# The low parts of a split float32 product stored as float16, with bfloat16 views of the weights

## The chip, the cores and the metric

The kernel runs on one core of one Trainium2 chip. The time is the device time of one execution in microseconds. The kernel before was run three times: 698.88 us in the median, 698.78 us the fastest and 699.11 us the slowest.

## The reference, cut to what matters

The input `x` has 2 x 1024 rows of 2048 numbers. Two residual steps follow each other, each a layer norm, a product with a 2048 x 2048 matrix and a gated add:

```python
x = x + tanh(g_xattn[0]) * matmul(fake_quant(layernorm(x)), fake_quant(ctx_4096))
y = layernorm(x)
y = concatenate([y[..., :1638], -4.0 * y[..., 1638:]], axis=-1)
x = x + tanh(g_ffn[0]) * scale * (y @ mask)        # mask: 2048 x 2048 of zeros and ones
```

The first product has operands of 8 bits (`fake_quant` rounds to 0..255). In the second product the left operand is float32 and has to keep more digits than one pass of TensorE gives; the right operand holds small whole numbers.

## The kernel before

Rows are taken in 16 tiles of 128 (`T`), 8 of each batch. Everything that is a matmul contracts 128 rows at a time and makes 128 x 512 numbers in PSUM.

**First product.** Both operands are float16 (lines 544 and 646 of the profile, `acc<-q,q1T`, `acc_M<-q,q1S` and the like). For batch 1 a part of it uses seven half-size products in place of eight.

**Second product.** Two row tiles t and u form a pair p, and there are eight pairs. A pair's normed rows are scaled (`scale2`, line 685), transposed on TensorE in float32 (`turn2`, line 692, four 128 x 128 transposes at a time) and taken out of PSUM as `A` (`take2`). The two tiles by the two halves of the contraction make a 2 x 2 block matrix, the mask likewise, and Winograd's form of Strassen's scheme replaces eight block products by seven, M1 to M7. The left sums are made in place (`combine`, lines 722 to 728), the right sums T1 to T4 are made once from the mask's bytes (`combine_w`, line 767) and kept in DRAM.

Each left operand is split in two: `part_hi` (line 738, ScalarE) rounds `A` to fp32r, the type that TensorE takes in one pass; `part_lo` (line 742, VectorE or GpSimd) stores `A - hi`, also as fp32r. `load_w` fetches a right block as bytes; `widen` (line 782, ScalarE) makes of each 128 x 1024 slice k an fp32r tile `wf`. Its values are whole numbers of at most a few bits.

`mm2` (line 809) does one slice k of one product for one pair. It issues four matmuls: hi with the left 512 columns of `wf`, hi with the right ones, lo with the left, lo with the right. All four add up in PSUM. So the second product is 7 products x 8 pairs x 8 slices x 4 = 1792 matmuls, 896 of them with hi and 896 with lo, in the order hi, hi, lo, lo. Only at the very end (the last four slices of the last pair, `tail`) the order is hi, lo, hi, lo. An fp32r matmul is one instruction that loads its own stationary operand; the profile still shows the load as a LDWEIGHTS row. A float16 matmul is two instructions, a Ldweights and a Matmult. `add2` (line 825) adds the result, times the factor `f2`, to the rows kept in DRAM, and `store2` writes them out.

**What sets the order.** The class `Plan` holds a list of all steps with estimated costs and due times; it simulates the engines and writes down an order for each. The steps are then issued in this order to TensorE, VectorE, ScalarE, GpSimd and the DMA queue of SyncE. The costs are constants in the code (4.2 for one `mm2`), and the change does not touch them. Pairs are taken two at a time (`ops_product2`), the second pair four slices behind the first, so that each `wf` serves two `mm2`, eight matmuls; the parts hi and lo of a product are made while the product before it runs.

**The factors.** `factor` (line 453) makes the layer norm's factor r = 1/sqrt(var + eps) of each row tile; the tiles of the second norm have v equal to "b". `f2` (line 381) is tanh(g_ffn) x scale.

Of the kernel before, what the change touches and what calls it, by code (L numbers as in the profile page):

```python
# [12 lines left out]
F32R = mybir.dt.float32r  # L13
F16 = mybir.dt.float16
BF = mybir.dt.bfloat16
# [3 lines left out]
ALU = mybir.AluOpType  # L19

P = 128
NB = 512
HB = 1024
EPS = 1e-5
UNIT = 2.0**-24
CENTER = 128.0
PAGES = 44

# [251 lines left out]
def gated_xattn_ffn_kernel(  # L280
# [29 lines left out]
    nc = tc.nc  # L310
# [9 lines left out]
    KH = KT // 2  # L320
# [19 lines left out]
    def page(shape, dtype, name: str):  # L340
        return pages.tile([P] + shape, dtype, tag="page", name=name)
# [8 lines left out]
    sc = const.tile([P, 7], F32, name="sc")  # L350
    nc.sync.dma_start(sc, scalars.partition_broadcast(P))
    gate = const.tile([P, 2], F32, name="gate")
# [8 lines left out]
    c1 = const.tile([P, 1], F32, name="c1")  # L361
    nc.vector.tensor_scalar(c1, z1, -1.0, CENTER, ALU.mult, ALU.add)
    c2 = const.tile([P, 1], F32, name="c2")
# [3 lines left out]
    f1u = const.tile([P, 1], F32, name="f1u")  # L367
    nc.vector.tensor_scalar(f1u, f1, 1.0 / UNIT, None, ALU.mult)
    f1c1u = const.tile([P, 1], F32, name="f1c1u")
# [7 lines left out]
    nc.vector.tensor_scalar(kc12d, f1c1, c2, float(K), ALU.mult, ALU.mult)  # L377
    nc.vector.tensor_scalar(kc12, c1, -CENTER, None, ALU.add)
    nc.vector.tensor_scalar(kc12, kc12, f1c2, float(K), ALU.mult, ALU.mult)
    f2 = const.tile([P, 1], F32, name="f2")  # L380
    nc.vector.tensor_scalar(f2, gate[:, 1:2], sc[:, 6:7], None, ALU.mult)

    ident = const.tile([P, P], F32, name="ident")
    make_identity(nc, ident)
# [56 lines left out]
    def factor(v, t: int):  # L441


        va, sd = root.pop((v, t))
        mean = mv[v, t][:, 0:1]
        r0 = small.tile([P, 1], F32, tag="r0", name=f"r0_{v}{t}")
        nc.vector.reciprocal(r0, sd)

        e = small.tile([P, 1], F32, tag="e", name=f"e_{v}{t}")
        nc.vector.tensor_scalar(e, r0, r0, va, ALU.mult, ALU.mult)  # L450
        nc.vector.tensor_scalar(e, e, -0.5, 1.5, ALU.mult, ALU.add)
        r = small.tile([P, 1], F32, tag="r", name=f"r_{v}{t}", bufs=T)
        nc.vector.tensor_scalar(r, r0, e, None, ALU.mult)
        fac[v, t] = (r, mean)
        if v == "a":
            w = small.tile([P, 1], F32, tag="w", name=f"w_{v}{t}")
            nc.vector.tensor_scalar(w, va, r, zs1, ALU.mult, ALU.mult)
            nc.vector.tensor_scalar(w, w, mean, None, ALU.subtract)
            nc.vector.tensor_scalar(r, r, rs1, None, ALU.mult)
            wr = small.tile([P, 1], F32, tag="wr", name=f"wr_{v}{t}")  # L460
            nc.vector.tensor_scalar(wr, w, r, None, ALU.mult)
            fac[v, t] = (r, w, wr)
# [42 lines left out]
    def take1(t: int, h: int, engine=None):  # L505
# [5 lines left out]
        if engine == "ACT":  # L511
            nc.scalar.activation(dst, v, AF.Copy, bias=-CENTER)  # L512
        else:
            nc.vector.tensor_scalar(dst, v, -CENTER, None, ALU.add)  # L514

# [159 lines left out]
    A, hi, lo, wt, wb, wr, wf, back, acc2 = ({} for _ in range(9))  # L675
# [54 lines left out]
    def left(m: str, p: int):  # L730

        t, u = 2 * p, 2 * p + 1
        return {"M1": (t, 0), "M2": (t, 1), "M3": (t, 1), "M4": (u, 1), "M5": (u, 0),
                "M6": (t, 0), "M7": (p, "S3")}[m]
# [3 lines left out]
        nc.scalar.copy(hi[m, p], A[left(m, p)])  # L738

    def part_lo(m: str, p: int, engine=None):  # L740
        lo[m, p] = page([KH, P], F32R, f"lo_{m}_{p}")
        engines[engine].tensor_sub(lo[m, p], A[left(m, p)], hi[m, p].bitcast(F32))  # L742


# [51 lines left out]
    def apart(p: int, m: str):  # L796

        return p == T // 2 - 1 and SUM[m] == "Y"

    def mm2(q: int, m: str, p: int, k: int, js=(0, 1)):  # L800
        if m in OPENS and k == 0 and apart(p, m):
            acc2[SUM[m], p] = [ps_tr.tile([P, NB], F32, tag="tr", name=f"acc2_{m}_{p}_{j}") for j in range(2)]
        elif m in OPENS and k == 0:
            acc = ps_acc.tile([P, 2, NB], F32, tag="acc", name=f"acc2_{m}_{p}")
            acc2[SUM[m], p] = [acc[:, j, :] for j in range(2)]
            acc2[SUM[m], p, 0] = flat(acc)
        for part in (hi, lo):
            for j in js:
                nc.tensor.matmul(  # L809
                    acc2[SUM[m], p][j],  # L810
                    part[m, p][:, k, :],
                    wf[q, m, k][:, ts(j, NB)],
                    start=(m in OPENS and k == 0 and part is hi),
                    stop=(k == KH - 1 and part is lo),
                    skip_group_check=True,
                )

    def load_back(p: int, i: int, h: int):
        back[p, i, h] = page([HB], F32, f"back_{p}_{i}_{h}")
        nc.sync.dma_start(back[p, i, h], kept[2 * p + i, h])  # L820
# [13 lines left out]
    def ops_norm(v: str, t: int, **when):  # L834
        name = lambda kind: ((kind + v, t), 0)
        op({"DVE": 2.0}, variance, v, t, writes=[name("v")], **when,
           reads=[(("bn" + v, t), c) for c in range(NC)])
        op({"ACT": 1.0}, square_root, v, t, reads=[name("v")], writes=[name("sd")], **when)
        op({"DVE": 8.0 if v == "a" else 4.0}, factor, v, t, reads=[name("sd")], writes=[name("r")], **when)
# [187 lines left out]
    def ops_parts(m: str, p: int):  # L1027
        a = ("A",) + left(m, p)
        op({"ACT": ACT(HB)}, part_hi, m, p, reads=both(a), writes=[(("hi", m, p), 0)],
           opens=[("page", ("hi", m, p))], lead=60)  # L1030
        op({"DVE": DV2(HB), "POOL": GPS(HB)}, part_lo, m, p, reads=[*both(a), (("hi", m, p), 0)],
           writes=[(("lo", m, p), 0)], opens=[("page", ("lo", m, p))], lead=60, port=True)
# [20 lines left out]
    def ops_product2(q: int, between):  # L1053
        pairs = (2 * q, 2 * q + 1)
        for n, m in enumerate(ORDER):
# [27 lines left out]
            for i, k, *js in steps:  # L1083
                p = pairs[i]
                js = js[0] if js else (0, 1)
                acc = ("acc2", SUM[m], p)
                two = apart(p, m)
                keys = [(acc + (j,), 0) if two else (acc, j) for j in js]
                opens = [("tr", acc + (j,)) for j in js] if two else [("acc", acc)]
                op({"PE": 2.1 * len(js)}, mm2, q, m, p, k, js, main=True, writes=keys,  # L1090
                   reads=[(("hi", m, p), 0), (("lo", m, p), 0), (("wf", q, m, k), 0)],
                   opens=opens if m in OPENS and k == 0 else [])
                if k == KH - 1:
                    for js2 in [(j,) for j in js] if two else [js]:
                        v = ("back", p) + TAKES[m]
                        keys = [(acc + (j,), 0) if two else (acc, j) for j in js2]
                        op({"DVE": DV2(len(js2) * NB)}, add2, m, p, js2, reads=keys, writes=[(v, j) for j in js2],
                           due=plan.place)
                        if m in LAST:
                            op({"SP": DMA}, store2, p, *TAKES[m], js2, reads=[(v, j) for j in js2], due=plan.place + 60)  # L1100
# [67 lines left out]
    for t in range(TPB, T):  # L1168
        v = ("x", t, 1)
# [60 lines left out]
```

## Time and profile before

| what | value |
|---|---|
| median of three runs | 698.88 us |
| span of the profiled execution, first to last instruction | 697.0 us |
| TensorE (PE) busy with matmuls | 674.0 us, 97% |
| VectorE, ScalarE, GpSimd busy | 490.2, 455.4, 316.8 us |
| granted TensorE clock | 1.000 over the whole span |
| second product's matmul rows | 1792 (896 hi, 896 lo) |
| first product's matmul rows (lines 544, 556, 574, 646) | 1036 |
| hi parts made (line 738) | 56, all on ScalarE |
| lo parts made (line 742) | 56: 30 on VectorE, 26 on GpSimd |

The page gives only the span of the profiled execution, not its time by the clock that the three runs use; the median stands 1.9 us above the span. A group row of the profile reads: line, engine, operation, output<-inputs, shape, count | busy microseconds, mean nanoseconds of one | idle time before them and who ended it. Matmuls are pipelined: a row's duration (389 ns for 512 columns) covers filling and draining, and the next one starts well before its end. What a matmul costs is therefore the distance from its start to the next start.

### The profile page before, as it was taken

The numbers are of one execution on the slowest core, as the hardware profiler recorded it, in microseconds if no ns is written. First come the engines' busy times: TensorE is split into PE (matmuls) and PEld (weight loads), VectorE is DVE, ScalarE is ACT, GpSimd is POOL, SyncE is SP. The second block draws the span as 40 slices with busy tenths as digits, with TensorE's granted clock in tenths as the row PEclk, the third lists the DMA queues.
The fourth block names the chain that finished last, engine by engine and source line by source line (L and its number), as shares of the span: only waits on it lengthen the run. The fifth ranks groups of instructions, "written<-read, shape, count | busy, mean of one in ns | idle before, by whom it ended". The sixth has DMA issues, their size and how long they took to land.

```text
span 697.0 us, 8833 instructions
## 1 busy us (share of the span) xinstructions
PE 674.0 (97%) x3180; PEld 471.7 (68%) x3180; DVE 490.2 (70%) x717; ACT 455.4 (65%) x536; POOL 316.8 (45%) x210
## 2 busy tenths in 40 slices
PE   1999999989999999999999999999999999999997
PEld 0444444468788888878885444447888888888885
DVE  6899958899998886497878888468572425583331
ACT  4599444286888566699926768229699347689540
POOL 8166789863625221855717887975120101040000
PEclk9999999999999999999999999999999999999999
DMA  8999406777995799477379677327074379155032
GB/s 302 393 393 380 162 13 231 259 261 251 361 400 225 233 324 339 140 247 278 120 263 330 222 268 245 121 92 275 27 260 162 105 231 324 67 170 222 22 131 90
DMA packets 63580, 155.78 MB, mean 223 GB/s; under 512 B 4912, under 2 KB 21296, under 8 KB 63536
## 3 DMA queue, kind: packets, MB, share of 16 engines
q1 hardware_dynamic: 63536, 155.21, 62.9%
q8 instruction: 25, 0.41, 0.2%
q14 instruction: 19, 0.16, 0.1%
HBM read 117.44 MB, written 37.75 MB: 223 GB/s over the span
## 4 chain that ended last, share of the span: by engine, by line
PE 87%; DMA 4%; DVE 4%; POOL 2%; ACT 2%; issue 1%; SPq 0%; ACTq 0%; DVEq 0%
PE acc_M L809 57%; PE acc L544 19%; PE acc_M L646 7%; PE tr L692 4%; DMA kv<-in_kv_dram 3%; DMA x<-in_x_dram 1%; POOL x L596 1%; DVE wB L767 1%; ACT wf_M L782 1%; POOL x L592 1%; PE tr L503 1%; DVE qn L472 0%; PE cs L574 0%; DVE x L685 0%; DVE bn_b L426 0%
## 5 line engine op out<-in xcount | busy, mean ns | idle before, releaser
L809 PE MATMUL acc_M<-wf_M,hi_M 128*128 128x512 f32 x896 | 282.0, 395 | 1.6 <-ACT wf_M L782 1.5
L809 PE MATMUL acc_M<-wf_M,lo_M 128*128 128x512 f32 x896 | 277.6, 390 | 0.6 <-POOL lo_M L742 0.6
L782 ACT ACTIVATE wf_M<-wr_M 128x1024 fp32r<-128x1024 uint8 x224 | 221.6, 1050 | 26.8 <-DMA wr_M<-in_wmask_dram 24.2
L809 PEld LDWEIGHTS acc_M<-wf_M,lo_M 128*128 128x128 f32 x896 | 168.0, 188 | 36.8 <-POOL lo_M L742 1.3
L809 PEld LDWEIGHTS acc_M<-wf_M,hi_M 128*128 128x128 f32 x896 | 164.1, 188 | 34.4 <-ACT wf_M L782 3.2
L544 PE MATMUL acc<-q,q1T 128*128 128x512 f16 x768 | 171.6, 381 | 1.2 <-DVE q1T L514 0.8
L825 DVE SCALAR_TENSOR_TENSOR back<-acc_M,f,back 128x1024 f32<-128x1024 f32 (+1 forms) x58 | 72.1, 1245 | 124.7 <-PE acc_M L809 117.1
L742 POOL TENSOR_TENSOR lo_M<-A,hi_M 128x1024 fp32r<-128x1024 f32 x24 | 62.1, 2586 | 179.5 <-ACT hi_M L738 160.1
L544 PEld LDWEIGHTS <-q1T 128*128 128x128 f16 x768 | 75.2, 98 | 90.2 <-issue 1.9
L592 POOL TENSOR_TENSOR x<-x,row 128x512 f32<-128x512 f32 x64 | 88.6, 1408 | 43.8 <-ACT sd_a L438 15.5
L596 POOL TENSOR_TENSOR x<-x,e 128x512 f32<-128x512 f32 x64 | 92.0, 1458 | 30.6 <-ACT e L586 16.1
L738 ACT CAST hi_M<-A 128x1024 fp32r<-128x1024 f32 x48 | 50.1, 1044 | 13.1 <-POOL A L726 4.7
L530 ACT ACTIVATE q<-kv,sc,rs 128x1024 uint8<-128x1024 f32 x45 | 53.5, 1236 | 7.8 <-DMA kv<-in_kv_dram 5.1
L586 ACT ACTIVATE e<-acc,tokb,f1u 128x512 f32<-128x512 f32 x34 | 25.1, 774 | 49.6 <-PE acc L544 47.8
L426 DVE BATCH_NORM_STATS2 bn_b<-x 128x6 f32<-128x512 f32 x64 | 43.1, 684 | 15.9 <-POOL x L596 15.6
L495 ACT COPY A<-tr 128x512 f32<-128x512 f32 x35 | 20.3, 584 | 46.5 <-PE tr L692 45.8
L742 DVE TENSOR_TENSOR lo_M<-A,hi_M 128x1024 fp32r<-128x1024 f32 x24 | 33.7, 1421 | 7.2 <-ACT hi_M L738 7.2
L568 DVE TENSOR_TENSOR pair<-pair,q 128x1024 f16<-128x1024 f16 x36 | 36.6, 1022 | 2.5 <-ACT q L530 0.8
L728 POOL TENSOR_TENSOR A<-A,A 128x1024 f32<-128x1024 f32 x8 | 21.1, 2648 | 23.7 <-DVE A L726 16.4
L522 POOL MEMSET q<- 128x1024 f32 x32 | 29.2, 952 | 5.1 <-DVE q L532 2.2
L512 ACT ACTIVATE q1T<-tr 128x1024 f16<-128x1024 uint8 x22 | 21.3, 1019 | 7.5 <-PE tr L503 6.8
L767 DVE SCALAR_TENSOR_TENSOR wB<-wB,wB 128x2048 uint16<-128x2048 uint16 x8 | 24.2, 3031 | 0.0
(103 smaller groups left out, 594.1 us busy)
## 6 DMA issues: line engine op xcount, KB each, us to landing
kv<-in_kv_dram SPq DMA_DIRECT2D x64, 512.0 KB, 9.2
x<-in_x_dram SPq DMA_DIRECT2D x32, 512.0 KB, 7.7
x<-x SPq DMA_DIRECT2D x32, 512.0 KB, 3.0
back<-x SPq DMA_DIRECT2D x32, 512.0 KB, 6.1
wr_M<-wt_T SPq DMA_DIRECT2D x32, 512.0 KB, 5.6
out_dram<-back SPq DMA_DIRECT2D x30, 512.0 KB, 3.6
wr_M<-in_wmask_dram SPq DMA_DIRECT2D x24, 512.0 KB, 5.4
n<-in_x_dram SPq DMA_DIRECT2D x16, 512.0 KB, 7.2
```

Of the source, the lines that this page charges most:

```text
L426: nc.vector.bn_stats(bn[v, t][:, c, :], xt[src[v, t, c // 2]][:, ts(c % 2, NB)])
L530: nc.scalar.activation(low, v, AF.Identity, bias=z2, scale=rs2)
L544: nc.tensor.matmul(acc1[b, c, tiles[0]][:, i, :], q1T[tiles[i]][:, k, :], rhs1(b, c, k), start=(k == 0), stop=(k == KT - 1),)
L568: nc.vector.tensor_add(colsum[b, c], colsum[b, c], v[:, i : i + 2, :])
L592: nc.gpsimd.tensor_add(xc, xc, colrow[b, c])
L596: nc.gpsimd.tensor_add(xc, xc, ev.pop((t, c)))
L646: nc.tensor.matmul(acc1[key][:, i, :], left_half(p, LEFT1[m])[:, 4 * s + k, :], right1(m, h, s)[:, k, :], start=(m in OPENS and s == 0 and ...
L738: nc.scalar.copy(hi[m, p], A[left(m, p)])
L742: engines[engine].tensor_sub(lo[m, p], A[left(m, p)], hi[m, p].bitcast(F32))
L782: nc.scalar.activation(wf[q, m, k], wr[q, m, k // 4][:, k % 4, :], AF.Copy, bias=-float(RIGHT[m][1]))
L809: nc.tensor.matmul(acc2[SUM[m], p][j], part[m, p][:, k, :], wf[q, m, k][:, ts(j, NB)], start=(m in OPENS and k == 0 and part is hi), stop= ...
L825: nc.vector.scalar_tensor_tensor(v, acc, f2, v, ALU.mult, ALU.add)
```

## The change

The lo part is stored as float16, and its matmuls take as moving operand the same `wf` tile seen as bfloat16: of each 4-byte number the upper two bytes. So the moving operand is read in steps of 4 bytes, 2 bytes at each step. The widened weights are whole numbers small enough to be the same in bfloat16. The hi part and its matmuls stay in fp32r. So that the small differences keep their digits in float16, the second norm's factor r is raised by 2^12 and `f2` lowered by as much; both are second operations in instructions that were there already.

```diff
+RAISE = 2.0**12
...
-    nc.vector.tensor_scalar(f2, gate[:, 1:2], sc[:, 6:7], None, ALU.mult)
+    nc.vector.tensor_scalar(f2, gate[:, 1:2], sc[:, 6:7], 1.0 / RAISE, ALU.mult, ALU.mult)
...
-        nc.vector.tensor_scalar(r, r0, e, None, ALU.mult)
+        if v == "b":
+            nc.vector.tensor_scalar(r, r0, e, RAISE, ALU.mult, ALU.mult)
+        else:
+            nc.vector.tensor_scalar(r, r0, e, None, ALU.mult)
...
-        lo[m, p] = page([KH, P], F32R, f"lo_{m}_{p}")
+        lo[m, p] = page([KH, P], F16, f"lo_{m}_{p}")
...
             for j in js:
+                w = wf[q, m, k] if part is hi else upper(wf[q, m, k])
                 nc.tensor.matmul(
                     acc2[SUM[m], p][j],
                     part[m, p][:, k, :],
-                    wf[q, m, k][:, ts(j, NB)],
+                    w[:, ts(j, NB)],
...
+    def upper(w):
+        return w.bitcast(BF).rearrange("p (n b) -> p n b", b=2)[:, :, 1]
```

On VectorE, ScalarE, GpSimd and the DMA queue of SyncE the changed program has the same instructions in the same order, with the same waits. On TensorE the matmuls stand in the same order too; in front of each of the 896 lo matmuls there is now a Ldweights of its own, and where a lo matmul waited for its part, the Ldweights now waits in the same place.

## The prediction

> **What bounds the kernel now.** I read the page's shares first, then who TensorE waits for, then the groups of the second product, then single stretches of the timeline where a float16 matmul stands between two fp32r ones.
>
> The page's busy times, its chain by line, and the groups that count:
>
> ```profile
> PE 674.0 (97%) x3180; PEld 471.7 (68%) x3180; DVE 490.2 (70%) x717; ACT 455.4 (65%) x536; POOL 316.8 (45%) x210
> ...
> L809 PE MATMUL acc_M<-wf_M,hi_M 128*128 128x512 f32 x896 | 282.0, 395 | 1.6 <-ACT wf_M L782 1.5
> L809 PE MATMUL acc_M<-wf_M,lo_M 128*128 128x512 f32 x896 | 277.6, 390 | 0.6 <-POOL lo_M L742 0.6
> ...
> L809 PEld LDWEIGHTS acc_M<-wf_M,lo_M 128*128 128x128 f32 x896 | 168.0, 188 | 36.8 <-POOL lo_M L742 1.3
> ...
> L544 PE MATMUL acc<-q,q1T 128*128 128x512 f16 x768 | 171.6, 381 | 1.2 <-DVE q1T L514 0.8
> ...
> L742 POOL TENSOR_TENSOR lo_M<-A,hi_M 128x1024 fp32r<-128x1024 f32 x24 | 62.1, 2586 | 179.5 <-ACT hi_M L738 160.1
> ```
>
> The reader is to see that TensorE is the bound (97%), that the second product waits 2.2 us in all (1.6 + 0.6), and that nothing but the pace of its own 1792 matmuls sets its length. The other engines have a third of their time to spare. So the change is worth what it does to the distance from one matmul's start to the next. The durations (395, 390, 381 ns) don't tell that; stretches of the chain do:
>
> ```profile
> 212.09 37.20 PE acc_M L809 x164
> ...
> 379.22 4.32 PE acc_M L646 x20
> ```
>
> 37.20/164 = 226.8 ns for an fp32r matmul in a long stretch, 4.32/20 = 216 ns for a float16 one. The 11 ns between them, times 896, is the 9.8 us that the change could bring at most if nothing else moved.
>
> But hi stays fp32r, so the kind changes every second matmul. The trace has this very pattern once, where two float16 matmuls of line 574 stand between fp32r pairs (the timeline; start, length, engine, count):
>
> ```profile
> 351.52 0.61 PE L809 MATMUL acc_M<-wf_M,lo_M 128*128 128x512 f32 x2
> ...
> 351.98 0.12 PEld L574 LDWEIGHTS <-ones_h 128*128 128x128 f16 x2 [0.26 <-issue]
> 351.98 0.61 PE L574 MATMUL cs<-pair,ones_h 128*128 128x512 f16 x2
> ...
> 352.21 0.41 PEld L809 LDWEIGHTS acc_M<-wf_M,hi_M 128*128 128x128 f32 x2
> 352.24 0.81 PE L809 MATMUL acc_M<-wf_M,hi_M 128*128 128x512 f32 x2
> ...
> 352.66 0.42 PEld L809 LDWEIGHTS acc_M<-wf_M,lo_M 128*128 128x128 f32 x2
> 352.89 0.62 PE L809 MATMUL acc_M<-wf_M,lo_M 128*128 128x512 f32 x2
> 353.12 0.41 PEld L809 LDWEIGHTS acc_M<-wf_M,hi_M 128*128 128x128 f32 x2
> 353.34 0.39 PE L809 MATMUL acc_M<-wf_M,hi_M 128*128 128x512 f32 x1
> ```
>
> Everywhere else a load begins 1 to 4 ns after the start of the matmul before it. The first float16 load does not: PEld is idle 0.26 us and the load begins at 351.976 (starts to the nanosecond are the trace's), 226 ns after the last fp32r matmul (351.750). The second begins at 351.991, when the first float16 matmul takes the array. So 15 ns of weight load lie bare. Line 646 shows the same at 366.942 and 366.957. In the other direction the fp32r load is early (352.208), and the first hi takes the array at 352.423 (its row starts early, at 352.24). From there the distances are 230 (to 352.653), 233 (to 352.886), 231 (to 353.117), 226 and from then on 227: after a change of kind, fp32r matmuls run slower for a while. After the float32 transposes of line 692 it is the same: 231, 236, 232 and the like, in place of 227.
>
> **The change, part by part.**
>
> *The lo matmuls, streaming.* 896 x 216 ns = 193.5 us, if a bfloat16 operand read in steps of 4 bytes streams like a contiguous float16 one. No row shows such an operand. Bounds: 216 (2 bytes per number, the float16 row) below; above, 227 to 231, the fp32r rows, which step through the same 4 bytes per number and read all of them. I take 216, since TensorE gets two bytes per number, as in the float16 rows; the upper bound adds 896 x 11 = 9.9 to 896 x 15 = 13.4 us. The Trainium skill, "SBUF — State Buffer", the note on cachelines, says that strides cost nothing while two accesses fall in one 16-byte line, and names up to 8 bfloat16 elements; by it the step of two is free and the term stays 193.5. No row here shows it.
>
> *The change of kind, fp32r to float16.* In TensorE's new order hi is followed by lo 452 times (444 as hi, hi, lo, lo, 8 at the end as hi, lo). Each lays bare a load: 452 x 15 ns = 6.8 us. Below: 0, if the load came early as among float16 matmuls (load 1 or 2 ns after the start before it). Both places in the trace show 15, so I take 15. The skill speaks for the 0: "TensorE: Matmul & The Clock Gate", Part 2, says that the queue pulls weight loads ahead of running matmuls when they go to the background buffer. By it alone the sum would be 6.8 us lower; the row with the 0.26 us idle is against it, and I go by the row.
>
> *The hi matmuls.* They never get to the settled pace: every pair follows a float16 pair. 230, 233, 231 are the distances after the float16 pair; mean 231.5: 896 x 231.5 = 207.4 us. Bounds: 227 (settled, 4.0 us less) and 236 (the slowest after transposes, 4.0 us more).
>
> *What these replace.* Over all starts of line 809, with seven stretches of waiting left out, the mean distance is 227.8 ns (1409 of 1784 lie at 226 or 227, the rest mostly at 230 to 237, after transposes): 1792 x 227.8 = 408.2 us.
>
> *The lo parts.* VectorE and GpSimd write 2 bytes per number in place of 4, from the same float32 inputs. VectorE's row is 1.22 us for one, GpSimd's 2.41 when it isn't held up; a float16 sum of float16 inputs (line 568) takes 0.69 on VectorE. So VectorE gains 0 to 0.5 us on each; for GpSimd no row has a float16 output, and I bound it at half and twice 2.41. The cover: each part is made during the product before it, some 14.5 us ahead; TensorE waited for one once, 0.56 us at 145.96, when the first product's last steps still run. Taken at 0; twice the time there would cost 2.4 us, half would give 0.56.
>
> *The rest.* The factors: a one-operation instruction of 128x1 (line 453, 214 ns) becomes a two-operation one (line 457, 272): 16 x 0.06 us on VectorE, and `f2` as much, under TensorE's work. The 896 Ldweights are a second instruction for TensorE's sequencer; the float16 stage issues such pairs at 216 ns, so 0. The wait for a lo part moves from the matmul to the Ldweights just ahead of it; behind it stand the same matmuls. Bytes and DMAs stay. ScalarE's `widen` (222 us of the two stages' 406) keeps ahead as long as TensorE isn't faster by more than a per cent or so: it held TensorE 1.5 us.
>
> *The sum.* 193.5 + 6.8 + 207.4 = 407.7 against 408.2: -0.5 us. The profiled span is 697.0 and the median 698.88, 1.9 us more; I take that as fixed. 697.0 - 0.5 + 1.9 = **698.4 us**. In one group of four: 216 + 216 + 231.5 + 231.5 + 15 = 910 ns against 4 x 227.8 = 911. The two things that float16 saves on the lo matmuls are given back at the seams. With the bounds of hi (4.0 either way) and of the lo parts (-0.6, +2.4), this case's own range is 693.8 to 704.8.
>
> **The rivals.**
>
> *The stride is paid* (slower). The lo matmuls stream at 227 to 231 ns, since they walk over the same addresses as fp32r. For it: fp32r's own 11 ns has no other visible reason than its 4 bytes per number, and a weight load after it doesn't begin before 226 ns, as if the stream itself took that long. Against it: only half of the bytes are taken. +9.9 to +13.4 on the sum: 708.3 to 711.8. It decides from 2 ns per lo matmul on (1.8 us, more than the 0.2% or 1.4 us that a measurement of this kernel can tell from no change).
>
> *The stride is paid dearly.* If the read fell to half pace, 432 ns, it would be 896 x 216 = 194 us more, 892 us. Nothing in the trace speaks for it and nothing excludes it.
>
> *The seams are free* (faster). Loads come early (-6.8) and hi settles at 227 (-4.0): down to 687.6. For one alone: 691.6 or 694.4. Against: the rows around 351.98 and 366.94.
>
> *It does nothing at all:* float16 runs at the pace of its neighbours. Then 698.9; by its number this can't be told from my forecast, but the rows would: lo at 227 without a seam.
>
> **How the numbers follow.** Chances: my case 0.45 (of which within 0.2% 0.25, faster 0.14, slower 0.06, by the spread of hi's pace); stride paid, in part or whole, 0.32; dearly 0.07; seams free 0.16. Faster: 0.14 + 0.13 = 0.27 (some of the last case is eaten by waits for `widen`); same: 0.25 + 0.03 = 0.28; slower: 0.06 + 0.32 + 0.07 = 0.45. The range leaves out the dear stride and the far end of the free seams: 693 to 711.
>
> **What would show it.** In the profile after: lo loads with f16 in their row and some 100 ns in place of 188; every first lo load beginning 226 to 236 ns after the second hi's start, the second one 15 ns later; a chain stretch of long runs of line 814 (the new place of 809) at 227 to 228 ns per matmul as before. Distances of 227 or more between the two lo matmuls would prove the stride's price; first lo loads 1 to 4 ns after a hi's start would prove the seams free. The prediction is wrong if TensorE waits for lo parts or `wf` by more than the 2.2 us of now, or if hi runs outside of 227 to 236 ns.

## The result, and the profile after

The changed kernel takes 706.83 us in the median of four runs (706.76 to 706.86) against 698.86 for the kernel before, in four runs too: a ratio of 1.0114 with a 95% interval of 1.01 to 1.0128. It is 8.0 us slower. Line 809 of before is line 814 now, 782 is 786, 742 is 746 and 692 is 696.

The page of the changed kernel, busy times and the groups that answer to those shown of before:

```profile
PE 681.5 (97%) x3180; PEld 355.2 (50%) x3180; DVE 495.6 (70%) x717; ACT 455.6 (65%) x536; POOL 315.8 (45%) x210
...
L814 PE MATMUL acc_M<-wf_M,hi_M 128*128 128x512 f32 x896 | 363.8, 487 | 1.4 <-ACT wf_M L786 1.4
L814 PE MATMUL acc_M<-wf_M,lo_M 128*128 128x512 bf16 x896 | 280.9, 393 | 0.6 <-POOL lo_M L746 0.6
...
L746 POOL TENSOR_TENSOR lo_M<-A,hi_M 128x1024 f16<-128x1024 f32 x24 | 61.1, 2548 | 180.5 <-ACT hi_M L742 164.5
...
L814 PEld LDWEIGHTS <-lo_M 128*128 128x128 f16 x896 | 52.1, 98 | 123.4 <-issue 121.1
```

The reader sees what did not go wrong. TensorE waits for `wf` and the lo parts 2.0 us, against 2.2 before. GpSimd makes a lo part as fast as before. The lo loads are short now, 98 ns. But PEld is idle 123.4 us in front of them, nearly all put down to "issue": the load had nothing to wait for that the profile shows. That is not lost time as such, since the hi matmuls stream meanwhile; what is lost is read from the starts below. The mean of hi, 487 ns, is no cost: after float16 a hi row starts some 200 ns before its matmul takes the array.

The whole second product, from each of its stretches' beginnings to its end, grew from 409.8 to 417.7 us: +7.9, all of the loss. The same long stretch of the chain as before:

```profile
213.03 38.01 PE acc_M L814 x164
```

38.01/164 = 231.8 ns per matmul, against 226.8. Within it, the timeline of TensorE (start, length, engine, line, operation, count):

```profile
230.96 0.62 PE L814 MATMUL acc_M<-wf_M,lo_M 128*128 128x512 bf16 x2
...
231.20 0.41 PEld L814 LDWEIGHTS acc_M<-wf_M,hi_M 128*128 128x128 f32 x2
231.22 0.82 PE L814 MATMUL acc_M<-wf_M,hi_M 128*128 128x512 f32 x2
...
231.88 0.12 PEld L814 LDWEIGHTS <-lo_M 128*128 128x128 f16 x2 [0.26 <-issue]
231.88 0.62 PE L814 MATMUL acc_M<-wf_M,lo_M 128*128 128x512 bf16 x2
...
232.12 0.41 PEld L814 LDWEIGHTS acc_M<-wf_M,hi_M 128*128 128x128 f32 x2
```

The lo load comes late each time, as at 351.98 in the profile before. By the starts in nanoseconds, the load of the first lo begins 224 or 234 ns after the second hi (231.651 to 231.875 here), the first lo takes the array 15 ns later (231.890), the second lo 227 ns after that, the next hi another 227 (not 216), and the second hi 229 after the first. 15 + 227 + 227 + 229 + 224 or 234 makes 922 or 932 ns for four, against 907 when all four were fp32r and settled.

### The profile page after: what moved, and what is told of

Same layout as the page of the kernel before. It is cut to its first block, busy times and chain, and to the rows that moved or that the text cites. A ratio compares the mean times of both kernels' runs of the same rounds, so it can differ in the third digit from the quotient of the medians.

```text
span 705.0 us, 8833 instructions
## 1 busy us (share of the span) xinstructions
PE 681.5 (97%) x3180; PEld 355.2 (50%) x3180; DVE 495.6 (70%) x717; ACT 455.6 (65%) x536; POOL 315.8 (45%) x210
## 4 chain that ended last, share of the span: by engine, by line
PE 89%; DMA 4%; DVE 4%; POOL 2%; issue 1%; ACT 1%; SPq 0%; ACTq 0%; DVEq 0%
PE acc_M L814 59%; PE acc L548 19%; PE acc_M L650 7%; PE tr L696 4%; DMA kv<-in_kv_dram 3%; DMA x<-in_x_dram 1%; POOL x L600 1%; DVE wB L771 1%; POOL x L596 1%; PE tr L507 1%; DVE qn L476 0%; PE cs L578 0%; DVE x L689 0%; DVE bn_b L427 0%; DVE bn_a L427 0%
## 5 line engine op out<-in xcount | busy, mean ns | idle before, releaser
L814 PE MATMUL acc_M<-wf_M,hi_M 128*128 128x512 f32 x896 | 363.8, 487 | 1.4 <-ACT wf_M L786 1.4
L814 PE MATMUL acc_M<-wf_M,lo_M 128*128 128x512 bf16 x896 | 280.9, 393 | 0.6 <-POOL lo_M L746 0.6
L746 POOL TENSOR_TENSOR lo_M<-A,hi_M 128x1024 f16<-128x1024 f32 x24 | 61.1, 2548 | 180.5 <-ACT hi_M L742 164.5
L814 PEld LDWEIGHTS <-lo_M 128*128 128x128 f16 x896 | 52.1, 98 | 123.4 <-issue 121.1
L572 DVE TENSOR_TENSOR pair<-pair,q 128x1024 f16<-128x1024 f16 x36 | 40.7, 1136 | 1.7
L746 DVE TENSOR_TENSOR lo_M<-A,hi_M 128x1024 f16<-128x1024 f32 x24 | 35.5, 1496 | 6.5 <-ACT hi_M L742 6.5
```

Source lines behind the costliest of these rows:

```text
L572: nc.vector.tensor_add(colsum[b, c], colsum[b, c], v[:, i : i + 2, :])
L814: nc.tensor.matmul(acc2[SUM[m], p][j], part[m, p][:, k, :], w[:, ts(j, NB)], start=(m in OPENS and k == 0 and part is hi), stop=(k == KH - ...
```

## The experiments

**One part alone: the step taken away.** The lo matmuls read the first half of the `wf` tile without a step.

```diff
-        return w.bitcast(BF).rearrange("p (n b) -> p n b", b=2)[:, :, 1]
+        return w.bitcast(BF)[:, 0:HB]
```

> The changed kernel, but each lo matmul reads 512 neighbouring bfloat16 numbers of the wf tile (its first half) in place of every second one, so what it multiplies is not the weights' upper bytes and the output is not the reference's; instructions and their order are the same. Theory S (the step of 4 bytes is what makes a lo matmul take 226.5 ns): lo falls to 216 ns, 896 x 10.5 = 9.4 us, and the time from 706.8 to 697.4; the bare load of 15 ns at each change of kind stays. Theory K (the neighbourhood of fp32r makes it slow) and theory M (float16 against bfloat16 makes it slow): lo stays at 226.5 and the time at 706.8.

Measured: 697.3 us, ratio 0.9979 to before, interval 0.997 to 0.9989. That is 9.5 us less than the changed kernel, as theory S had it, and theories K and M fall. The timeline of TensorE shows lo at 216 with the late load still there:

```profile
225.46 0.81 PE L814 MATMUL acc_M<-wf_M,hi_M 128*128 128x512 f32 x2
226.11 0.12 PEld L814 LDWEIGHTS <-lo_M 128*128 128x128 f16 x2 [0.27 <-issue]
226.11 0.61 PE L814 MATMUL acc_M<-wf_M,lo_M 128*128 128x512 bf16 x2
226.34 0.19 PEld L814 LDWEIGHTS acc_M<-wf_M,hi_M 128*128 128x128 f32 x1
```

The first lo takes the array at 226.123 (load at 226.108, 15 ns before), the second at 226.341, 218 ns later; the median over all pairs is 215.

**Fewer changes of kind.** Every second step takes lo before hi.

```diff
-        for part in (hi, lo):
+    turn = [0]
...
+        turn[0] += 1
+        opens = m in OPENS and k == 0
+        ends = k == KH - 1
+        for part in ((lo, hi) if turn[0] % 2 == 0 and not opens and not ends else (hi, lo)):
```

> The changed kernel with every second step taking lo before hi (except the first and last slice of a sum), so that hi is followed by lo 268 times in place of 452. If each such place costs a bare weight load of 15 ns: 184 x 15 = 2.8 us less, 704.0. If the places cost nothing of their own: 706.8. If hi also runs slower only because it always stands behind a lo pair, up to 184 x 2 x 2.5 = 0.9 us more come off.

Measured: 704.0 us (703.9 to 704.01), 2.8 us under the changed kernel for 184 seams fewer: 15 ns for each, which is what the timeline shows of one. No further gain for hi. The idle time of PEld before lo loads is 117.6 us in all, hardly less than the 123.4 of the changed kernel. What falls with the seams is the part put down to "issue", from 121.1 to 73.4, a ratio of 0.61 where the seams have 268/452 = 0.59:

```profile
L819 PEld LDWEIGHTS <-lo_M 128*128 128x128 f16 x896 | 65.8, 97 | 117.6 <-issue 73.4
```

**No change of kind at all.** hi is float16 too, and both parts read the stepped view.

```diff
-RAISE = 2.0**12
+RAISE = 2.0**6
...
-        hi[m, p] = page([KH, P], F32R, f"hi_{m}_{p}")
+        hi[m, p] = page([KH, P], F16, f"hi_{m}_{p}")
...
-        engines[engine].tensor_sub(lo[m, p], A[left(m, p)], hi[m, p].bitcast(F32))
+        engines[engine].tensor_sub(lo[m, p], A[left(m, p)], hi[m, p])
...
-                w = wf[q, m, k] if part is hi else upper(wf[q, m, k])
+                w = upper(wf[q, m, k])
```

> hi is float16 too (the factor is 2^6 in place of 2^12, so that hi stays in float16's range), and both hi and lo read the stepped bfloat16 view: no change of kind inside the second product. Theories S and M: 1792 x 226.5 = 405.9 us in place of the changed kernel's 416.2 (408.2 + 8.0): 696.5. Theory K: without fp32r the lo matmuls and the hi ones run at 216, 387.1: 677.7.

Measured: 694.99 us, ratio 0.9946 (0.9931 to 0.9961); 696.5 was expected. Nearly every distance between two of its matmuls is 225 to 227 ns, and loads are early again: in the timeline the second hi starts at 560.846 and the lo load 2 ns later, at 560.848.

```profile
560.62 0.61 PE L814 MATMUL acc_M<-wf_M,hi_M 128*128 128x512 bf16 x2
560.85 0.32 PEld L814 LDWEIGHTS <-lo_M 128*128 128x128 f16 x2
561.07 0.61 PE L814 MATMUL acc_M<-wf_M,lo_M 128*128 128x512 bf16 x2
561.30 0.32 PEld L814 LDWEIGHTS <-hi_M 128*128 128x128 f16 x2
```

So the step costs as much without an fp32r neighbour as with one.

**Both kinds the same, and no step.** As the last, with the weights widened to a bfloat16 tile. Nothing of the computation is left out.

```diff
-        wf[q, m, k] = page([HB], F32R, f"wf_{q}_{m}_{k}")
+        wf[q, m, k] = page([HB], BF, f"wf_{q}_{m}_{k}")
...
-                w = upper(wf[q, m, k])
+                w = wf[q, m, k]
```

> As e3, but the weights are widened to a bfloat16 tile and read without steps. Theory S: 1792 x 216 = 387.1 us in place of 416.2: 677.7, or up to 5 more if the widening on ScalarE, 222 us under 387, begins to hold TensorE up. Theory M: 226.5 stays, 696.5. Theory K: 677.7.

Measured: 679.39 us (679.34 to 679.44), ratio 0.9723 to before, interval 0.9708 to 0.9737. This beats both kernels: 19.3 us under the one before, measured beside it at 698.73. A group of its page, and a stretch of the chain first of the stepped version, then of this one:

```profile
L786 ACT ACTIVATE wf_M<-wr_M 128x1024 bf16<-128x1024 uint8 x224 | 221.0, 1046 | 23.3 <-DMA wr_M<-in_wmask_dram 20.8
```

```profile
248.59 1.81 PE acc_M L814 x8
```

```profile
245.41 1.73 PE acc_M L814 x8
```

226 ns against 216. `widen` takes as long into bfloat16 as into fp32r, and TensorE waits for it 3.4 us, against 1.4 in the changed kernel; that fits the 1.7 us between the 677.7 expected and the 679.4 measured. (In the profiles of this and some other experiments a matmul row in fifty or so is missing, so that the mean over a long stretch comes out some 2% high; short whole stretches and the median distance are used.)

**The price of a step.** Steps of four, eight and three bfloat16 numbers, all from the version with both parts float16. The column halves read the same numbers, so the outputs are not the reference's. The line `w,` of the first diff below belongs to all three.

```diff
-        return w.bitcast(BF).rearrange("p (n b) -> p n b", b=2)[:, :, 1]
+        return w.bitcast(BF).rearrange("p (n b) -> p n b", b=4)[:, :, 1]
...
-                    w[:, ts(j, NB)],
+                    w,
```

```diff
-        return w.bitcast(BF).rearrange("p (n b) -> p n b", b=2)[:, :, 1]
+        return w.bitcast(BF).rearrange("p (n b) -> p n b", b=8)[:, :, 1].unsqueeze(1).to_broadcast([P, 2, NB // 2])
```

```diff
-        return w.bitcast(BF).rearrange("p (n b) -> p n b", b=2)[:, :, 1]
+        return w.bitcast(BF)[:, 0 : 3 * NB].rearrange("p (n b) -> p n b", b=3)[:, :, 1]
```

> As e3 (hi and lo float16, 695.0 us, 226 ns per matmul), but the moving operand takes every fourth bfloat16 number, 8 bytes apart, over the whole wf tile, the same for both column halves; the output is not the reference's. Theory L (the price goes with the 16-byte lines touched: 64 without steps, 128 with a step of two, 256 here): 216 + 3 x 10.5 = 247.5 ns, 1792 x 21 = 37.6 us more than e3, 732.6. Theory T (any step costs the same once): 695.0.

> As e5 with every eighth number, 16 bytes apart; the tile holds 256 of them, which are read twice in a row. Each number is then in a line of its own. Theory L: 512 lines, 216 + 7 x 10.5 = 289.5 ns, 1792 x 63 = 113 us more than e3, 808. Theory T: 695.0. The Trainium skill (SBUF — State Buffer, the note on cachelines) has a penalty begin when no second access falls in the same line: by it this run alone, of the four, pays much, and e5 is still at 695.

> As e5 with every third bfloat16 number, 6 bytes apart, over the first three quarters of the wf tile; the output is not the reference's. Theory B (the moving operand comes at some 9.05 bytes of address span per ns and partition, whatever part of them is used; e3 226, e5 452, e6 900 ns): 512 x 6 / 9.05 = 339.5 ns, 1792 x 113 = 203 us more than e3, 898. If steps are rounded up to powers of two: as e5, 1097.

Measured, one run each: 1097.1, 1925.1 and 891.1 us. Both L and T fell at the first two: the price neither stays nor grows by 10.5 ns for each 64 lines; from a step of two on it doubles with the step. The note on cachelines of the Trainium skill ("SBUF — State Buffer") differs too: a step of four puts two numbers into each 16-byte line, and it cost 402 us more than the step of two. The third run was made for the theory that came out of this, B, and held it (898 expected). Stretches of the chain, for steps of four, eight and three:

```profile
344.94 5.42 PE acc_M L814 x12
```

```profile
1612.93 187.18 PE acc_M L814 x208
```

```profile
345.81 6.74 PE acc_M L814 x20
```

| moving operand | bytes it walks over | ns per matmul | bytes per ns |
|---|---|---|---|
| float16 or bfloat16, no step | 1024 | 216 | 4.7 |
| step of two | 2048 | 226 | 9.06 |
| fp32r (before) | 2048 | 226.7 | 9.03 |
| step of three | 3072 | 337 | 9.12 |
| step of four | 4096 | 452 | 9.06 |
| step of eight | 8192 (4096, twice) | 900 | 9.10 |

Per partition, a stepped moving operand comes at 9.0 to 9.1 bytes of address span per nanosecond, used or not. The first row is set by something else: at this rate its 1024 bytes would take 113 ns, and it takes 216, a pace that goes with the columns (256 of them take 109 ns, below). At 4 bytes per number the rate gives 226 ns, 5% over that pace. fp32r fits the same rate, but no run varied it by itself. In the run with the step of eight the granted clock was 0.50 over its long stretch, as the clock row of its page has it, in tenths (9 stands for 0.9 and more):

```profile
PEclk9995555555555555555589855555555555555555
```

The rate does not hang on that clock: in two short stretches the second product ran there at a granted clock of 1.00, with starts at 145.632, 146.532 and 147.430, and at 565.079, 565.979 and 566.879. These are 898 to 900 ns apart, as they are at 0.50.

**Per matmul or per column?** Each matmul of the two float16 versions cut in two of 256 columns.

```diff
-                nc.tensor.matmul(
-                    acc2[SUM[m], p][j],
+                for i in range(2):
+                    nc.tensor.matmul(
+                        acc2[SUM[m], p][j][:, ts(i, NB // 2)],
...
-                    w[:, ts(j, NB)],
+                        w[:, ts(2 * j + i, NB // 2)],
...
```

> As e3 (step of two), with each matmul cut in two of 256 columns, 3584 in all. If the price of the step is one per matmul (10.5 ns however short): 3584 x (106.7 + 2.5 + 10.5) = 429 us in place of 405.9, 718. If it goes with the columns (5.25 ns for 256): 410 us, 699.

> As e4 (no step, 679.4 us), cut the same way: the scale for e7. 3584 x (106.7 + 2.5) = 391.4 us in place of 387.1: 683.7, by both theories, if weight loads stay hidden at 109 ns.

Measured, one run each: 696.65 and 683.23 us; the distances are 113.3 and 109.2 ns, by a stretch of the chain of each:

```profile
504.82 70.72 PE acc_M L815 x624
```

```profile
497.97 68.12 PE acc_M L815 x624
```

The price goes with the columns: 1024 bytes in 113.3 ns is 9.04 per ns. It is no cost of starting.

**Why the lo load is late.** From the version without a step, lo loads and makes only 64 columns.

```diff
-                    acc2[SUM[m], p][j],
-                    part[m, p][:, k, :],
+                    acc2[SUM[m], p][j][: P if part is hi else P // 2],
+                    part[m, p][:, k, : P if part is hi else P // 2],
```

> As e1 (hi fp32r, lo float16 without step, 697.3 us), but lo loads and makes 64 columns of its 128, so half of the lo sums are left out and the output is not the reference's. It asks why the first lo load comes late. Theory W (a float16 load after an fp32r matmul has to wait for that matmul's end): it comes late here too, and if 64 columns load slower than 128 did, the bare 15 ns grow, by up to 40 ns, 452 x 40 = 18 us: 697 to 715. Theory F (only the fast load of 128 float16 columns can't run beside an fp32r stream, and 64 columns load another way): it comes early, the 15 ns go, 452 x 15 = 6.8 us: 690.5.

Measured: 830.35 us, outside of both. In this run loads wait on both sides, before the 64 columns of lo and before the 128 of hi. In the timeline of loads both kinds stand idle now:

```profile
300.14 0.14 PEld L814 LDWEIGHTS <-lo_M 128*64 128x64 f16 x2 [0.36 <-issue]
300.69 0.30 PEld L814 LDWEIGHTS acc_M<-wf_M,hi_M 128*128 128x128 f32 x2 [0.41 <-issue]
301.35 0.14 PEld L814 LDWEIGHTS <-lo_M 128*64 128x64 f16 x2 [0.36 <-issue]
```

Four matmuls take 1210 ns (300.142 to 301.352) in place of some 914. Only the width of lo differs from the version without a step, so these 297 ns or so go with it; whether the change of width or the narrow load by itself costs them was not varied. As the width changes at each seam too, the run does not tell the theories apart. It stays open why a float16 load does not come early behind an fp32r matmul. That it isn't the stream's bytes is likely, since the stepped bfloat16 stream has the same 2048 bytes and loads come early under it, but no run isolated it.

## Why the prediction was wrong

It was wrong in one term, and its sum said no change (-0.5 us) where the kernel became 8.0 us slower. What happened is the rival "the stride is paid", which held 0.32 against 0.45 for the main case; the time lies inside the range (693 to 711) only because the range had been widened for the rivals, and a little under that rival's own 708.3 to 711.8, since hi came out cheaper.

- **What bounds the kernel: right.** TensorE's own pace, in the second product alone: +7.9 us there, +8.0 in all.
- **The lo matmuls, streaming: wrong.** "I take 216, since TensorE gets two bytes per number." They ran at 226.7: 896 x 10.7 = +9.6 us. The cause is shown: with the step taken away they run at 215 to 216, and 9.5 us come off. What failed in the prediction is the choice of the nearest row: with 2048 bytes spanned by either operand it was fp32r (226.8), not float16 (216), and the price goes with the bytes spanned, not with those used. The rival had this row. Its other sign, that after an fp32r matmul the next load did not begin before 226 ns, "as if the stream itself took that long", was weaker than it looked: under the stepped stream, which takes 226 ns too, float16 loads come early. The Trainium skill's note on cachelines, cited in the prediction, is not borne out by the steps of two, three and four, each of which puts at least two numbers into a 16-byte line.
- **The change of kind: right in place and size.** 15 ns were expected and 15 found in the timeline; 184 fewer of them gave 2.8 us, 15.2 each. The Trainium skill's rule that the queue pulls loads ahead ("TensorE: Matmul & The Clock Gate", Part 2) holds among float16 matmuls here (109 and 216 ns distances with loads 1 or 2 ns after a start); from fp32r to float16 no load was pulled ahead (most began 224 or 234 ns after a start).
- **The hi matmuls: right in kind, a little off in size.** 231.5, the mean of the first two distances (230 and 233), was expected from one place; from 417.7 less about 2 of waiting, less lo (203.1) and seams (6.9), 205.7 remain, 229.6 each: -1.7 us. That is within the bounds given (227 to 236).
- **The lo parts, the factors, the second instruction: right, nothing.** 1.22 and 2.40 us for a lo part on VectorE and GpSimd; waits as before.
- **The sum.** -0.5 expected; + 9.6 for the step - 1.7 for hi = +7.4, where 8.0 was measured. The 0.6 us between them are what the prediction's term for the fp32r matmuls of before had too much: 408.2, where 409.8 less 2.2 of waiting makes 407.6. As hi's 229.6 is itself what remained, that the sum closes is no further proof. With the step's term right, the rest stood: the version without a step was measured at 697.3 where 698.4 was predicted.

## What to carry to other kernels

Price a stepped moving operand by the bytes that its addresses span, not by the bytes that are used, wherever that comes to more than the pace by columns (216 ns for 512 here): at some 9.05 bytes per ns and partition, a 16-bit view with a step of two was as slow as the 32-bit tile it looks into. Where both kinds of matmul alternate, look for a place in the trace where they already do, and count the seams. The gain that the change was after came, and more, once both parts were 16 bits wide and the weights were written narrow in the first place, at no cost to the engine that writes them.

## What was not expected of the hardware

- Steps cost in proportion to the span, with none of them free beside the 216 ns without a step: 226, 337, 452 and 900 ns for 512 columns at steps of 4, 6, 8 and 16 bytes.
- With the step of eight TensorE was busy 99% of the time and yet the granted clock fell to 0.50 for most of the run; the 900 ns for a matmul were the same at 1.00 and at 0.50.
- A lo part of 64 stationary columns between hi parts of 128 cost about 300 ns in each group of four matmuls; whether it is the change of width or the narrow load was not shown.
